# More gathered rows through ACT's DMA queue, in smaller blocks behind its long operations: a graph attention layer on Trainium2

## The chip, the cores and the metric

The kernel runs on one core of one Trainium2 chip. The metric is the device time of one execution in microseconds (us). PE is the matrix engine (PEld its weight loads), DVE the vector engine, ACT the scalar engine, POOL the general-purpose engine, SP the engine that issues most of the DMAs. ACT and POOL issue DMAs too, from their own instruction queues. A name with a q behind it (ACTq, SPq, POOLq) is the sequencer of that engine, which issues DMAs and loads registers.

## The reference

A graph has 12,500 nodes with 128 features and 200,000 edges, sorted by their destination. The layer normalizes the features and applies a relu (h), scores each edge, keeps at most the 16 best edges of each destination, and adds the messages of those with softmax weights:

```
h = relu(layernorm(x))
score = sum((h @ W_Q.T)[dst] * (h @ W_K.T)[src]) / sqrt(128) * exp(-edge_weight)
keep the 16 highest scores of each dst;  alpha = softmax of the kept ones by dst
agg[dst] += alpha * (h[src] @ W_msg.T)
out = x + relu(h @ W_self.T + agg)
```

All data are 32-bit floats or integers; the sources of the edges are random.

## The kernel before

**Tiles.** The edges stand in their order in chunks of 128, one edge to a partition. Fourteen chunks make a window (`GC = 14`), and there are 112 windows (`G`). A window's edges belong to a short run of nodes, so that the work between edges and nodes is done with one-hot matrices: `to_e` (nodes to edges), `opo` (places of an edge in its node's list of slots and in the window). A prologue normalizes x into the table `h_tab` in DRAM and prepares the indices.

**Rows of the sources.** Each edge needs the row of `h_tab` that belongs to its source, 512 bytes. They come by three ways:
- POOL gathers a whole chunk, 128 rows, with one indirect DMA (L183) into `hs`, a tile of a window with 8 buffers. `let_go` (L219) copies the chunk's indices on DVE and calls the gather; `more(k)` deals these calls out over a pass, two chunks each.
- SP takes chunk 13 of some windows, row by row, one DMA of 512 bytes each, 36 rows a pass (`SP_ROWS`), into `lateSP`.
- ACT takes chunk 12 of some windows in the same way, `ACT_ROWS` rows a pass, into `lateACT`. The chunks that these two streams take are fixed at build time: a stream with a rate of r rows a pass takes as many whole chunks as it can have ready in time. They are taken from POOL's work.

The row streams have two steps. `rows_named` loads up to 16 row numbers at a time into registers (L791). It is a generator: its body runs only as the loop over it asks for the next value. `rows_asked(name, n)` issues the next n DMAs (L803) from the numbers named so far. `all_landed` lets DVE wait for a chunk.

**The loop.** Pass i works on several windows at once, each in another stage, in an order written out by hand; the instructions of each engine run in that order. What this document speaks of:
- `far_of` (PE L602, ACT L604), four blocks, for window i+1. Its products lie in the one buffer "a" of PSUM, so each block's matmul waits for ACT to have read the block before. `to_edges` (ACT L609) makes `to_e` of it.
- `edges_turned` and `away` (PE L615 and L625, ACT L618 and L627), three blocks of `aw` in the same buffer, and `places` (ACT L631), which makes `opo`.
- `q_to_edges` (PE L642) and `scores` (DVE L653), four blocks of a window, window i.
- `slots_by_node` (PE L667 and L669) of window i-1, `best` (DVE from L683 on, the 16 best), `sum_of_exps` (ACT L700) and `kept_to_edges` (PE L712) of window i-2.
- `on_edges` (DVE L718 to L725), `exps` (ACT L729), `weights` (DVE L733, L734), then `sums` (PE L744, two halves) of window i-3, `sums_out` (ACT L749, tile `agn`), and for i-4 and i-5 the products, the output (DVE L764) and the store (SP L770).

A buffer of `hs` is free for a later window when the sums of its window are done.

Of the kernel before, what the change touches and what calls it, by code (L numbers as in the profile page):

```python
# [19 lines left out]
ACT = mybir.EngineType.Activation  # L20

SP_ROWS = 36
ACT_ROWS = 24
PSUM = bass.MemoryType.PSUM

P = 128
# [55 lines left out]
def gnn_layer(  # L82
# [106 lines left out]
    AT_ONCE = 16  # L189
    STREAMS = {"SP": (nc.sync, SP, -1, SP_ROWS, GC - 1), "ACT": (nc.scalar, ACT, 3, ACT_ROWS, GC - 2)}  # L190
    NLATE = 4
# [19 lines left out]
    def let_go(g, k):  # L211

        js = [j for j in range(2 * k, min(2 * k + 2, own[g])) if (g, j) not in slow]
        if k == 0:
            T[g]["ix"] = rows_pool.tile([P, GC], I32, name="ix", bufs=7)
        if not js:
            return
        ix, j0, j1 = T[g]["ix"], js[0], js[-1] + 1
        nc.vector.tensor_copy(ix[:, j0:j1], idx_all[:, GC * g + j0:GC * g + j1])  # L219
        gather(g, j0, j1, lambda j: ix[:, j:j + 1])  # L220
# [32 lines left out]
    def raw_stats(g):  # L253
        T[g]["raw"] = row_stats(rows_pool, T[g]["hs"], own[g], f"r{g % 2}")
# [5 lines left out]
    def raw_begun(g):  # L260
        normed(T[g]["hs"], 0, 1, *T[g]["raw"])

    def raw_finished(g, part):
        rows, (rs, sm) = T[g]["hs"], T[g]["raw"]
        if part < 3:
            normed(rows, 1 + 3 * part, 4 + 3 * part, rs, sm)
            return
        for t in range(10, own[g]):
            nc.vector.tensor_scalar(rows[:, t, :], rows[:, t, :], rs[:, t:t + 1], sm[:, t:t + 1],
                                    op0=OP.mult, op1=OP.add)  # L270
            nc.vector.tensor_scalar(rows[:, t, :], rows[:, t, :], 0.0, None, op0=OP.max)
# [256 lines left out]
    def softmax_rest(pool, v16):  # L528

        top = pool.tile([P, 1], F32, name="top")  # L530
        nc.vector.tensor_scalar(top, v16[:, 0:1], FLOOR, None, op0=OP.max)
        nm = pool.tile([P, 1], F32, name="nm")
        nc.vector.tensor_scalar(nm, top, -1.0, None, op0=OP.mult)
        e16 = pool.tile([P, TOPK], F32, name="e16")
        den = pool.tile([P, 1], F32, name="den")
        nc.scalar.activation(e16, v16, AF.Exp, bias=nm, accum_out=den)
        rden = pool.tile([P, 1], F32, name="rden")
        nc.vector.tensor_scalar(rden, den, 0.25, None, op0=OP.max)
        nc.vector.reciprocal(rden, rden)
        return top, e16, rden  # L540


    with tc.tile_pool(name="win", bufs=2) as win:
# [25 lines left out]
        def load_x(g):  # L569
            k = G - TAIL  # L570
            if g == k:
                starts(g, 1, TAIL, XT)
            T[g]["x_t"] = rows_pool.tile([P, D], F32, name="x_t", bufs=8)
            if g < k:
                nc.sync.dma_start(T[g]["x_t"], x[ds(T[g]["start", 0], P), :])
            else:
                nc.sync.dma_start(T[g]["x_t"], x_end[ds(T[g]["start", 1], P), :])
# [204 lines left out]
        def rows_named(name, i):  # L782

            _, engine, _, _, _ = STREAMS[name]
            todo = rows_at.get((name, i), [])
            while todo:
                g, j, e = todo[0]
                n = 1
                while n < min(AT_ONCE, len(todo)) and todo[n][:2] == (g, j):
                    n += 1  # L790
                _, numbers = nc.values_load_multi_w_load_instructions(  # L791
                    late_b[g:g + 1, j - GC + 2, e:e + n], engines=[engine], min_val=0, max_val=ROW * (N - 1),
                    skip_runtime_bounds_check_because="nodes' numbers times a row's bytes")
                ready[name] += [(g, j, e + k, st) for k, st in enumerate(numbers)]
                yield
                todo = todo[n:]

        def rows_asked(name, most=1000):
            for g, j, e, st in ready[name][:most]:
                m = slow[g, j][1]  # L800
                if e == 0:
                    T[g]["late", j] = win.tile([P, D], F32, name=f"late{name}", bufs=NLATE)
                d = STREAMS[name][0].dma_start(T[g]["late", j][e:e + 1, :].bitcast(U8), h_bytes[ds(st, ROW)])  # L803
                d.then_inc(landed[name][m % NLATE], 16)
                tc.no_tile_sem_insts.add(d.ins.name)
                tc.add_to_no_dep_group(f"rows{g}_{j}", d.ins)
            del ready[name][:most]
# [6 lines left out]
        def at(g, stage, *args):  # L814
            if 0 <= g < G:
                stage(g, *args)


        for i in range(-3, G - 1):
            at(i + 3, load_nodes)  # L820
            for k, _ in enumerate(rows_named("SP", i)):
                rows_asked("SP")
                if k == 0:
                    at(i - 1, load_x)
            if not rows_at.get(("SP", i)):
                at(i - 1, load_x)
            if i == G - 2:
                load_x(G - 2)
                load_x(G - 1)
            if i == 8:  # L830
                nc.sync.dma_start(h_tab[N:N + P, :], zpad)
                nc.sync.dma_start(x_end[XT:XT + P, :], zpad)
                nc.sync.dma_start(x_end[0:XT, :], x[N - XT:N, :])
            def raw(part):
                if i in (1, 2):
                    raw_finished(i + 1, part)

            def more(k):

                if i in (-1, 0, 1):  # L840
                    g = i + 6
                else:
                    g, k = (i + 4, k + 2) if k < 5 else (i + 5, k - 5)
                    if g < 8:
                        return
                if i >= -1 and g < G:
                    let_go(g, k)

            at(i, q_to_edges, 0)
            at(i - 5, output)  # L850
            at(i - 5, store)
            at(i - 3, weights)
            more(0)
            at(i - 4, sums_turned)
            at(i + 1, far_of, 0)
            at(i - 4, sums_turned_out)
            at(i + 1, q_out)
            at(i, q_to_edges, 1)
            at(i + 1, far_of, 1)
            rows_asked("ACT", ACT_ROWS // 8)  # L860
            raw(0)
            for b in range(3):
                at(i - 1, slots_by_node, b)
            at(i + 1, far_of, 2)
            more(1)
            at(i - 2, best)
            more(2)
            at(i - 2, sum_of_exps)
            at(i - 1, slots_out)
            raw(1)  # L870
            at(i, q_to_edges, 2)
            at(i + 1, far_of, 3)
            raw(2)
            at(i + 2, h_turned)
            at(i, scores, 0)
            more(3)
            at(i + 1, to_edges)
            rows_asked("ACT", ACT_ROWS * 5 // 16)
            at(i + 2, h_turned_out)
            at(i - 2, kept_to_edges)  # L880
            at(i - 1, node_by_slots)
            at(i + 1, edges_turned)
            at(i - 3, sums, 0)
            at(i, scores, 1)
            more(4)
            at(i + 1, away, 0)
            at(i, q_to_edges, 3)
            at(i - 2, one_over_sum)
            at(i + 1, away, 1)
            rows_asked("ACT")  # L890
            at(i - 3, sums, 1)
            at(i, scores, 2)
            at(i - 2, on_edges)
            more(5)
            at(i + 1, away, 2)
            at(i - 3, sums_out)
            at(i - 4, products)
            at(i - 2, exps)
            at(i + 1, places)
            for _ in rows_named("ACT", i + 1):  # L900
                pass
            rows_asked("ACT", ACT_ROWS * 3 // 8)
            at(i, scores, 3)
            at(i, scores_in_slots)
            if i == 0:
                raw_stats(2)
                raw_stats(3)
                raw_begun(2)
                raw_begun(3)
            if i in (1, 2):  # L910
                raw_finished(i + 1, 3)
            more(6)
            at(i + 2, q_made)
            if i > 0 and later:
                later.pop(0)()
# [92 lines left out]
    with tc.tile_pool(name="gen", bufs=1) as gen, tc.If(nc.values_load(  # L1008
# [116 lines left out]
        with tc.For_i(0, NT, 1) as T:  # L1125
# [16 lines left out]
            _, e16, rden = softmax_rest(gen, cand[:, 0:TOPK])  # L1142
# [40 lines left out]
```

## Time and profile before

| | us |
|---|---|
| median of 3 runs | 3100.45 |
| lowest and highest run | 3090.87, 3109.37 |
| profiled execution, its own time | 3112.28 |
| its span from the first to the last instruction | 3110.5 |

| in the profiled execution | count |
|---|---|
| gathers of POOL from `h_tab` | 1456 |
| row DMAs of SP, of ACT | 3968, 2560 |

The mean granted clock of PE is 0.741. Rows of a timeline give the start in us, the duration in us, engine, line, operation, tiles, shapes and count, and in brackets the idle time before it with what ended it. "issue" there is time in which the engine waited for nothing that the profile shows, "remote" an event that the profile can't put down to an instruction. Instructions of a sequencer aren't counted as busy time of its engine.

### The profile page before, as it was taken

How to read it: one execution, taken by the hardware profiler on the slowest of the kernel's cores; microseconds unless marked ns; L12 is line 12 of the kernel's file. 1: busy time of each engine (PE TensorE's matmuls, PEld its weight loads, DVE VectorE, ACT ScalarE, POOL GpSimd, SP SyncE). 2: the span in 40 equal slices, each digit the busy share in tenths (PEclk: the TensorE clock that was granted, in tenths of full speed). 3: DMA queues.
4: the chain of work that ended last, by engine and by line, in shares of the span. 5: the costliest groups of instructions: out<-in, count | busy, mean ns of one | idle time of the engine just before them, and what ended most of it. 6: DMA issues, size and time to landing. Idle time of an engine off the chain costs nothing. (4 is left out here: it accounts for less than half of the span.)

```text
span 3110.5 us, 55712 instructions
## 1 busy us (share of the span) xinstructions
PE 2052.1 (66%) x13800; PEld 1692.2 (54%) x13801; DVE 1264.1 (41%) x7016; ACT 1041.8 (33%) x2190; POOL 1457.7 (47%) x1529
## 2 busy tenths in 40 slices
PE   0256666666677667676676666776676666667667
PEld 0145555555555555555565555555565555555556
DVE  4453334433344334443433333434434433344346
ACT  4443323333333233333333333333333332333333
POOL 6524444444444444444444445444445444444440
PEclk9867777767777776777777777767767777777779
DMA  8201111111111111111111111111111111111110
GB/s 218 62 24 43 50 43 42 43 39 44 43 42 44 42 44 42 43 42 42 44 44 42 42 43 44 42 40 43 44 44 44 43 42 42 44 43 41 42 40 12
DMA packets 113004, 144.38 MB, mean 46 GB/s; under 512 B 36775, under 2 KB 86567, under 8 KB 111904
## 3 DMA queue, kind: packets, MB, share of 16 engines
q0 software_dynamic: 48512, 99.39, 12.6%
q1 hardware_dynamic: 59038, 40.04, 4.7%
q8 instruction: 109, 1.79, 0.2%
q14 instruction: 225, 1.84, 0.2%
q10 hardware_dynamic: 5120, 1.32, 0.2%
HBM read 126.79 MB, written 14.40 MB: 45 GB/s over the span
## 5 line engine op out<-in xcount | busy, mean ns | idle before, releaser
L183 POOL DMA_INDIRECT hs<-h_tab,ix x1456 | 1394.9, 958 | 1540.6 <-PE e L744 605.4
L744 PEld LDWEIGHTS e<-hs,alz 128*128 128x128 f32 x3142 | 612.1, 296 | 291.9 <-issue 280.5
L744 PE MATMUL e<-hs,alz 128*128 128x128 f32 x3142 | 668.9, 393 | 0.0
L642 PE MATMUL q<-q,to_e 128*128 128x128 f32 x3348 | 589.9, 324 | 44.9 <-issue 42.9
L642 PEld LDWEIGHTS q<-q,to_e 128*128 128x128 f32 x3348 | 545.9, 234 | 121.5 <-issue 87.5
L604 ACT ACTIVATE far<-a,minus 128x512 bf16<-128x512 f32 (+1 forms) x447 | 294.6, 659 | 891.9 <-issue 344.2
L653 DVE SCALAR_TENSOR_TENSOR prod<-hs,dec_all,q 128x128 f32<-128x128 f32 x1623 | 470.2, 342 | 133.6 <-remote 60.1
L602 PE MATMUL a<-rel,ident 112*128 112x512 bf16 (+1 forms) x447 | 211.0, 472 | 426.0 <-issue 264.4
L627 ACT ACTIVATE aw<-a 128x400 bf16<-128x400 f32 x336 | 169.4, 504 | 836.7 <-PE a L625 450.4
L683 DVE TENSOR_SCALAR ell<-slots,e 128x40 f32<-128x40 f32 x112 | 27.9, 249 | 933.6 <-remote 390.2
L625 PE MATMUL a<-minus_at,pdT 32*128 32x400 bf16 x336 | 146.6, 436 | 376.1 <-ACT aw L627 245.4
L669 PE MATMUL e<-opo,sl 128*41 128x40 f32 x3348 | 236.9, 252 | 34.0 <-issue 33.9
L669 PEld LDWEIGHTS e<-opo,sl 128*41 128x41 f32 x3348 | 215.7, 168 | 43.5 <-issue 31.3
L667 PEld LDWEIGHTS <-zrow 1*41 1x41 bf16 x112 | 11.3, 101 | 412.3 <-issue 412.2
L609 ACT ACTIVATE to_e<-far 128x1920 f32<-128x1920 bf16 x112 | 201.3, 1797 | 3.4
L764 DVE SCALAR_TENSOR_TENSOR o<-s,x_t 128x128 f32<-128x128 f32 x112 | 32.6, 291 | 403.2 <-ACT up L729 350.1
L625 PEld LDWEIGHTS <-pdT 32*128 32x128 bf16 x336 | 31.4, 94 | 190.5 <-ACT pdT L618 122.9
L631 ACT ACTIVATE opo<-aw 128x1200 f32<-128x1200 bf16 x112 | 134.7, 1202 | 0.1
L653 DVE DVE_READ_ACCUMULATOR prod<-hs,dec_all,q 128x1 f32 x1623 | 132.0, 81 | 0.0
L219 DVE COPY ix<-idx_all 128x2 int32<-128x2 int32 (+1 forms) x747 | 126.1, 183 | 0.0
L712 PEld LDWEIGHTS <-to_e 128*128 128x128 bf16 x1674 | 68.0, 111 | 94.4 <-DVE km L695 88.0
L712 PE MATMUL x<-km,to_e 128*128 128x43 bf16 x1674 | 76.7, 202 | 58.4 <-DVE km L695 58.3
(197 smaller groups left out, 1868.0 us busy)
## 6 DMA issues: line engine op xcount, KB each, us to landing
lateSP<-h_tab SPq DMA_DIRECT2D x3968, 0.5 KB
lateACT<-h_tab ACTq DMA_DIRECT2D x2560, 0.5 KB
hs<-h_tab,ix POOLq DMA_INDIRECT x1456
h_r<-h_tab SPq DMA_DIRECT2D x112, 64.0 KB
x_t<-in_x_dram SPq DMA_DIRECT2D x108, 64.0 KB
out_dram<-o SPq DMA_DIRECT2D x108, 64.0 KB
xg<-in_x_dram SPq DMA_DIRECT2D x2, 1400.0 KB
h_tab<-xg SPq DMA_DIRECT2D x2, 1400.0 KB
```

What stands on the lines that cost most here:

```text
L183: nc.gpsimd.indirect_dma_start(out=T[g]["hs"][:, j, :], out_offset=None, in_=table[0:N, :], in_offset=bass.IndirectOffsetOnAxis(ap=index(j ...
L602: nc.tensor.matmul(pr[:, 0:n1 - n0], lhsT=upper(ident[0:RR, g:g + 1]).to_broadcast([RR, P]), rhs=rel[:, n0:n1], start=True, stop=True)
L604: nc.scalar.activation(T[g]["far"][:, n0:n1], pr[:, 0:n1 - n0], AF.Square, bias=minus)
L609: nc.scalar.activation(T[g]["to_e"][:, 0:n], T[g]["far"][:, 0:n], AF.Relu, bias=1.0, scale=-1.0)
L625: nc.tensor.matmul(pr[:, 0:400], lhsT=T[g]["pdT"], rhs=minus_at.rearrange("k w j s -> k (w j s)")[:, n0:n1], start=True, stop=True)
L627: nc.scalar.activation(T[g]["aw"][:, n0:n1], pr[:, 0:400], AF.Square)
L631: nc.scalar.activation(T[g]["opo"].rearrange("e w j s -> e (w j s)"), T[g]["aw"], AF.Relu, bias=1.0, scale=-1.0)
L642: nc.tensor.matmul(pq[:, (j - j0) * P:(j - j0 + 1) * P], lhsT=T[g]["to_e"][:, j * P:(j + 1) * P], rhs=T[g]["q"], start=True, stop=True)
L653: nc.vector.scalar_tensor_tensor(prod, rows_of(g, j), dec_all[:, c:c + 1], T[g]["pq", b][:, (j % 4) * P:(j % 4 + 1) * P], op0=OP.mult, op1 ...
L669: nc.tensor.matmul(et[0:KM + 1, STEP * j:STEP * j + WN], lhsT=sl1[g % 2][:, j, :], rhs=T[g]["ow"][:, j, :], start=False, stop=(j == n - 1))
L712: nc.tensor.matmul(px[:, j, 0:KM + 3], lhsT=upper(T[g]["to_e"][:, j * P:(j + 1) * P]), rhs=upper(T[g]["km"]), start=True, stop=True)
L744: nc.tensor.matmul(T[g]["pa"], lhsT=alz[g % 2][:, WW * j + PRE:WW * j + PRE + P], rhs=rows_of(g, j), start=(j == 0), stop=(j == n - 1))
```

## The change

`ACT_ROWS` goes from 24 to 40. In the loop, the calls of `rows_asked("ACT", ...)` are dealt out anew; the numbers are ACT's row DMAs at each place of a pass:

| place in ACT's order | before | after |
|---|---|---|
| behind `far`, block 0 | 0 | 3 |
| behind `far`, block 1 | 3 | 3 |
| behind `far`, block 2 | 0 | 3 |
| behind `to_e` | 7 | 7 |
| behind `aw`, block 0 | 0 | 3 |
| behind `aw`, block 1 | 5 (all that are left) | 3 |
| behind `aw`, block 2 | 0 | 3 |
| behind `opo` and the loads of the next numbers | 9 | 15 |

```diff
-ACT_ROWS = 24
+ACT_ROWS = 40
...
             at(i + 1, far_of, 0)
+            rows_asked("ACT", 3)
             at(i - 4, sums_turned_out)
             at(i + 1, q_out)
             at(i, q_to_edges, 1)
             at(i + 1, far_of, 1)
-            rows_asked("ACT", ACT_ROWS // 8)
+            rows_asked("ACT", 3)
...
             at(i + 1, far_of, 2)
+            rows_asked("ACT", 3)
             more(1)
...
             at(i + 1, to_edges)
-            rows_asked("ACT", ACT_ROWS * 5 // 16)
+            act_names = rows_named("ACT", i + 1)
+            rows_asked("ACT", 7)
...
             at(i + 1, away, 0)
+            rows_asked("ACT", 3)
...
             at(i + 1, away, 1)
-            rows_asked("ACT")
+            rows_asked("ACT", 3)
...
             at(i + 1, away, 2)
+            rows_asked("ACT", 3)
             at(i - 3, sums_out)
             at(i - 4, products)
             at(i - 2, exps)
             at(i + 1, places)
-            for _ in rows_named("ACT", i + 1):
+            for _ in act_names:
                 pass
-            rows_asked("ACT", ACT_ROWS * 3 // 8)
+            rows_asked("ACT", ACT_ROWS - 25)
```

## The prediction

> **What bounds the kernel now.** I read the page first, then the busy time of two stretches, then the waits by engine, and last the timeline of single passes, because the page's averages name no bound: no engine is busy for more than two thirds.
>
> ```profile
> span 3110.5 us, 55712 instructions
> PE 2052.1 (66%) x13800; PEld 1692.2 (54%) x13801; DVE 1264.1 (41%) x7016; ACT 1041.8 (33%) x2190; POOL 1457.7 (47%) x1529
> 1519.00:1546.50 27.50, 18.37 (x124) 15.29 (x123) 10.65 (x61) 8.68 (x19) 13.43 (x15) 0.75 0.16 40
> 3020.20:3038.20 18.00, 14.34 (x127) 12.12 (x124) 9.57 (x52) 8.70 (x18) 0.00 (x0) 0.88 0.07 17
> ```
>
> The last two rows are two stretches, each one pass of the main loop (us, then busy time and count of PE, weight loads, DVE, ACT and POOL, then granted clock, DMA share and GB/s). Both hold the same matrix, vector and scalar work and both issue 24 rows on ACT. The first also has POOL's gathers and lasts 27.5 us, the second comes after the last gather and lasts 18.0. So a pass is longer than its work by what goes on around the gathers. The waits (engine, line, what it waited for, us in total, times, longest) say where:
>
> ```profile
> POOL hs L183 <- PE e L744: 605.4, 99, 7.9
> POOL hs L183 <- issue: 370.0, 1210, 0.6
> DVE ell L683 <- remote: 390.2, 44, 9.9
> ACT far L604 <- issue: 344.2, 126, 4.3
> DVE ell L683 <- PE a L602: 267.9, 30, 9.2
> DVE ell L683 <- PE e L669: 225.9, 29, 9.4
> PEld L667 <- issue: 412.2, 111, 5.7
> PE a L602 <- ACT far L604: 161.2, 106, 17.2
> ```
>
> POOL itself waits, for a buffer that the sums (L744) free, so it isn't the bound by its own rate. But `best` (L683), with which the second half of a pass begins on DVE, is often released by something other than the matmuls it needs (L669): 74 of 103 times in these three rows. And PE waits some 3.7 us in each pass ahead of L667 (412.2 over 111), after its L602 has waited for ACT's `far`. One pass shows both:
>
> ```profile
> 1504.56 0.95 POOL L183 DMA_INDIRECT hs<-h_tab,ix  x1 [7.72 <-PE e L744]
> 1505.19 0.51 ACT L627 ACTIVATE aw<-a 128x400 bf16<-128x400 f32 x1 [3.65 <-PE a L625]
> 1505.59 0.36 ACT L749 ACTIVATE agn<-e,rden 128x128 f32<-128x128 f32 x1
> 1505.94 1.20 ACT L631 ACTIVATE opo<-aw 128x1200 f32<-128x1200 bf16 x1
> 1507.77 3.27 ACTq L803 DMA_DIRECT2D lateACT<-h_tab  x9
> 1508.70 7.56 SPq L803 DMA_DIRECT2D lateSP<-h_tab  x12
> 1511.09 0.69 ACT L604 ACTIVATE far<-a,minus 128x512 bf16<-128x512 f32 x1 [3.94 <-issue]
> 1511.83 0.38 PE L602 MATMUL a<-rel,ident 112*128 112x512 bf16 x1 [3.53 <-ACT far L604]
> 1512.30 2.32 PE L669 MATMUL e<-opo,sl 128*41 128x40 f32 x30
> 1513.60 0.94 POOL L183 DMA_INDIRECT hs<-h_tab,ix  x1 [0.30 <-issue]
> 1516.26 0.25 DVE L683 TENSOR_SCALAR ell<-slots,e 128x40 f32<-128x40 f32 x1 [8.64 <-PE a L602]
> 1518.66 0.94 POOL L183 DMA_INDIRECT hs<-h_tab,ix  x1 [4.11 <-DVE prod L653]
> ```
>
> Two chains leave from about 1504.5, where the sums end. On POOL, eight gathers start at 1504.56, 1.25 us apart, the eighth ending at 1514.54; `best` starts 1.72 us after that. On ACT, `aw`, `agn`, `up`, `opo`, then two loads of row numbers and nine row DMAs, and only then `far` at 1511.09; PE's L602 waits for that `far`, and L669 follows and ends at 1514.62. The gathers' chain ends last, by 1.64 us. From `best` on, a second burst of up to six gathers starts (1518.66), and the next sums stand behind it. Where there are no gathers, ACT's chain ends last:
>
> ```profile
> 3026.88 0.50 ACT L627 ACTIVATE aw<-a 128x400 bf16<-128x400 f32 x1 [1.75 <-PE a L625]
> 3027.28 0.36 ACT L749 ACTIVATE agn<-e,rden 128x128 f32<-128x128 f32 x1
> 3027.63 1.20 ACT L631 ACTIVATE opo<-aw 128x1200 f32<-128x1200 bf16 x1
> 3029.37 2.90 ACTq L803 DMA_DIRECT2D lateACT<-h_tab  x9
> 3032.32 0.69 ACT L604 ACTIVATE far<-a,minus 128x512 bf16<-128x512 f32 x1 [3.48 <-issue]
> 3033.53 1.48 PE L669 MATMUL e<-opo,sl 128*41 128x40 f32 x30
> 3035.05 0.25 DVE L683 TENSOR_SCALAR ell<-slots,e 128x40 f32<-128x40 f32 x1 [6.05 <-PE e L669]
> ```
>
> Here `best` starts 0.04 us after L669, and `far` 0.05 us after the ninth DMA (3029.37 + 2.90 = 3032.27). So ACT's compute instruction stands behind the whole block of issues in its queue.
>
> **The change part by part.** Rows on ACT go from 24 to 40 a pass. ACT's stream takes one whole chunk (128 rows) at a time: 20 chunks now (2560 rows), 33 after (4224).
>
> *What POOL loses.* Thirteen gathers of 1456. One costs 0.96 us busy and 0.31 us of issue (370.0 over 1210), and they fall in the second burst, which is on the path: 13 x 1.26 = 16 us less in all. DVE loses a copy or a part of one with each; it idles there.
>
> *Rows placed under long operations.* Three behind the first `far`, three (as now) behind the second, three behind the third, seven (as now) behind `to_e`, three behind the first `aw`, three instead of five behind the second. A row costs 2.90/9 = 0.32 us of ACT's queue. Behind the first `far`, `aggT`, `q` and the second `far` start up to 0.3 us later; PE has L669 to do meanwhile, so nothing. Behind the third, the next on ACT is the exponential that needs `best`'s result, later than three rows take. Behind the first two `aw`, PE has q's block and the second half of the sums. All these I cost at nothing; should the cover go, three rows are 0.96 us a pass.
>
> *Three rows behind the last `aw`.* Ahead of `agn`, `up` and `opo`, with no matmul that hides it: `agn` now starts 0.40 us after `aw` (3026.88 to 3027.28), then not before three rows are issued, 0.95 us. Term A: +0.5 us on ACT's chain. DVE's `kept` and `o` wait for `up` and move with it, well ahead of their use on PE (the next sums).
>
> *The block behind `opo`.* The numbers are still loaded there, since the generator that holds the loads runs only when the loop over it does. Forty numbers in loads of at most 16 are three loads, not two, and then 15 DMAs, not nine.
>
> ```profile
> L791 ACTq TENSOR_LOAD <-late_b x213: 551/1041/1241, 215.0 to 3045.1; - x107
> ```
>
> The row is one line's durations in ns (min/median/max). The longer ones overlap `opo`, so the third load costs near the minimum. Term B: +0.6. Six more DMAs at 0.32: term C, +1.9.
>
> *Rows that fall into the gathers' flight.* With A to C the block ends some 9.5 us after the burst's start instead of 6.5. In that stretch, issues can be slow:
>
> ```profile
> 2131.85 3.46 ACTq L803 DMA_DIRECT2D lateACT<-h_tab  x3
> 3033.53 0.83 ACTq L803 DMA_DIRECT2D lateACT<-h_tab  x3
> 2129.47 9.36 SPq L803 DMA_DIRECT2D lateSP<-h_tab  x16
> 2131.84 1.37 PE L669 MATMUL e<-opo,sl 128*41 128x40 f32 x30
> 2136.37 0.25 DVE L683 TENSOR_SCALAR ell<-slots,e 128x40 f32<-128x40 f32 x1 [8.14 <-remote]
> ```
>
> Three rows behind the second `far`, issued while a burst was in flight, took 3.46 us; with no burst 0.83. SP pays 0.58 to 0.63 a row there (9.36/16, 7.56/12), against 0.32. So the block's last rows, four or five of them, cost more. Bounds for term D: 0 and 2.6 us (3.46 - 0.83). I take 1.4, five rows at SP's surplus of 0.28, which is about the middle, as the fast and the slow case both occur.
>
> *The sum.* A + B + C + D = 0.5 + 0.6 + 1.9 + 1.4 = 4.4 us later `far`, and so L669. Of that the gathers' chain already covers what L669 now waits for in vain: 1.64 us in the pass of 1504, 3.16 in that of 2131 (2136.37 - 2133.21), none in the 29 waits that end with L669. Three quarters at 2.4 make 1.8; I take 1.7. Net 2.7 us a pass. POOL's first burst doesn't move against the sums, and its second follows `best`, so the whole of it goes into the period. Forty rows a pass run in 105 passes. The last gather starts at 3018.9, so three of them have no burst: there A + B + C = 3.0 counts whole. 102 x 2.7 + 3 x 3.0 - 16 = 275 + 9 - 16 = +268 us. The profiled execution took 3112.3 us for its span of 3110.5, 0.4% over the median of 3100.45, inside the runs' spread; 3100 + 268 gives **3370 us** as forecast (3112 + 268 = 3380 against the profile).
>
> [...] The trace agrees that L669 comes at two prices, 2.32 us (1512.30) and 1.48 (3033.53). [...]
>
> **The rivals.** *The block is not slowed* (D = 0). For it: ACT's nine rows of 1507.77 were issued at 0.36 while SP paid 0.63. Against: the 3.46. Then 1.3 net: 102 x 1.3 + 9 - 16 = +126, 3225 us.
>
> *The burst holds all late rows* (D = 2.6). For it: SP is slow in every burst shown. Against: the same block of three cost 0.83 without one. Net 3.9: 102 x 3.9 - 7 = +391, 3490 us; L669 at 2.32 instead of 1.48 where it is fast now could add a few tens of us.
>
> *Issues cost ACT nothing, and the gathers decide* (faster). If ACT's compute instructions could be taken up while its queue issues DMAs, neither the third load nor the six rows would hold `far`; the gathers' chain would keep ending last, and 13 gathers fewer would be the whole effect: 3100 - 16 = 3084 us. It decides as soon as `far` comes no later than the 1.6 us of slack. Against it: `far` at 3032.32 right behind the ninth issue, and 126 waits of `far` put down to issue. [...]
>
> *It doesn't move the path* (no change): the rows' cost just fills the slack, 1.7 us, and the gathers' saving stays small. A + B + C alone are 3.0, so this needs half of them hidden.
>
> **How the numbers follow.** Forecast 0.70, rows not slowed 0.11, rows held 0.12, gathers decide 0.04, no change 0.03. The range runs from the first rival's price, 3225, to 3520, 30 us beyond the second's for L669's slower price; it leaves out the cases at and below no change (0.07) and the far ends. A difference of 0.5% (16 us) is about what a measurement of this kernel can tell from none. Slower by more than that: 0.93; within: 0.03; faster: 0.04.
>
> **What would show it.** In the changed profile: ACT's block behind `opo` has 15 issues and takes 5 to 8 us (now 3); `far` starts some 4 us later after the first gather of its burst, near 11 us instead of 6.5; PE's wait ahead of L667 roughly doubles from 3.7 us a pass; `best` is released by L669, not later than it; the first burst's eight gathers stay 1.25 us apart; a pass lasts about 30 us. Wrong would be: `far` starting before the block has been issued, `best` still 1.7 to 2 us behind the eighth gather with L669 long done, or a period that grew while that block didn't.

## The result: slower, 3543 us for 3099

| | before | after |
|---|---|---|
| median, us | 3098.74 | 3543.01 |
| lowest and highest run, us | 3090.87, 3109.37 | 3533.71, 3566.31 |
| profiled execution: its time, its span, us | 3112.28, 3110.5 | 3566.31, 3564.6 |
| gathers from `h_tab` | 1456 | 1443 |

The ratio is 1.1442, 95% interval 1.1373 to 1.1512. The change makes the kernel slower, as forecast, but by 444 us where 268 were forecast; 3543 lies 23 us above the range.

The changed kernel's page, two lines of it:

```profile
span 3564.6 us, 59136 instructions
PE 1911.8 (54%) x13800; PEld 1593.3 (45%) x13801; DVE 1273.6 (36%) x7012; ACT 1069.6 (30%) x2190; POOL 1447.9 (41%) x1516
```

No engine works much longer than before: ACT 28 us more, DVE 10, PE 140 less. The time has gone into waits. The waits of the changed kernel (engine, line, what it waited for, us in total, times, longest):

```profile
DVE ell L683 <- PE e L669: 1345.0, 108, 13.7
PEld L667 <- issue: 1041.6, 111, 11.1
...
PE a L602 <- ACT far L604: 950.4, 107, 14.6
ACT far L604 <- issue: 942.4, 110, 10.0
```

`best` (L683) is now released by L669 108 times; before it was 29. PE's wait ahead of L667 has gone from 3.7 to 9.4 us a pass (1041.6 over 111), and `far` waits 942 us for ACT's own issues, before 344. One pass of the changed kernel's timeline:

```profile
1712.55 0.95 POOL L183 DMA_INDIRECT hs<-h_tab,ix  x1 [6.09 <-PE e L744]
1712.81 0.50 ACT L627 ACTIVATE aw<-a 128x400 bf16<-128x400 f32 x1 [3.16 <-PE a L625]
1712.88 0.83 ACTq L803 DMA_DIRECT2D lateACT<-h_tab  x3
1713.75 0.37 ACT L749 ACTIVATE agn<-e,rden 128x128 f32<-128x128 f32 x1 [0.44 <-issue]
...
1714.12 1.19 ACT L631 ACTIVATE opo<-aw 128x1200 f32<-128x1200 bf16 x1
...
1716.15 8.44 SPq L803 DMA_DIRECT2D lateSP<-h_tab  x12
...
1716.92 8.06 ACTq L803 DMA_DIRECT2D lateACT<-h_tab  x15
...
1721.39 0.95 POOL L183 DMA_INDIRECT hs<-h_tab,ix  x1 [0.30 <-issue]
...
1725.03 0.69 ACT L604 ACTIVATE far<-a,minus 128x512 bf16<-128x512 f32 x1 [9.72 <-issue]
...
1726.53 2.32 PE L669 MATMUL e<-opo,sl 128*41 128x40 f32 x30
...
1728.89 0.25 DVE L683 TENSOR_SCALAR ell<-slots,e 128x40 f32<-128x40 f32 x1 [13.49 <-PE e L669]
```

The eighth gather ends at 1722.34, as early after the first as before. The block of 15 is issued until 1724.98, `far` follows 0.05 us later, and `best` comes 0.04 us behind L669 (1726.53 + 2.32 = 1728.85). ACT's chain ends last now.

Means over the passes that have a burst of eight gathers (96 before, 97 after; all 104 of each give the same within 0.03), worked out from the rows of the timelines, in us:

| | before | after |
|---|---|---|
| last `aw` to `agn` | 0.40 | 0.95 |
| end of `opo` to ACT's first row | 0.60 | 1.60 |
| the block behind `opo` | 3.02 | 7.32 |
| first gather to `far` | 6.21 | 12.09 |
| end of L669 to `best` (what L669 waits for in vain) | 1.78 | 0.04 |
| first gather to `best` | 11.78 | 15.94 |
| period | 26.87 | 31.24 |

### The profile page after: what moved, and what is told of

Read it like the earlier page. It is cut to its first block, busy times and chain, and to the rows that moved or that the text cites. A ratio compares the mean times of both kernels' runs of the same rounds, so it can differ in the third digit from the quotient of the medians.

```text
span 3564.6 us, 59136 instructions
## 1 busy us (share of the span) xinstructions
PE 1911.8 (54%) x13800; PEld 1593.3 (45%) x13801; DVE 1273.6 (36%) x7012; ACT 1069.6 (30%) x2190; POOL 1447.9 (41%) x1516
## 5 line engine op out<-in xcount | busy, mean ns | idle before, releaser
L602 PE MATMUL a<-rel,ident 112*128 112x512 bf16 (+1 forms) x447 | 221.5, 496 | 996.3 <-ACT far L604 950.4
L744 PEld LDWEIGHTS e<-hs,alz 128*128 128x128 f32 x3116 | 509.6, 253 | 253.7 <-issue 245.9
L642 PE MATMUL q<-q,to_e 128*128 128x128 f32 x3348 | 565.9, 322 | 0.0
L744 PE MATMUL e<-hs,alz 128*128 128x128 f32 x3116 | 561.7, 347 | 0.0
L642 PEld LDWEIGHTS q<-q,to_e 128*128 128x128 f32 x3348 | 537.9, 234 | 43.0 <-issue 22.3
L683 DVE TENSOR_SCALAR ell<-slots,e 128x40 f32<-128x40 f32 x112 | 27.9, 249 | 1348.9 <-PE e L669 1345.0
L667 PEld LDWEIGHTS <-zrow 1*41 1x41 bf16 x112 | 12.1, 108 | 1041.7 <-issue 1041.6
L669 PE MATMUL e<-opo,sl 128*41 128x40 f32 x3348 | 254.7, 267 | 0.0
L669 PEld LDWEIGHTS e<-opo,sl 128*41 128x41 f32 x3348 | 238.3, 185 | 14.7
L618 ACT CAST pdT<-a 32x128 bf16<-32x128 f32 x112 | 28.5, 254 | 226.8 <-remote 225.0
L725 DVE TENSOR_REDUCE kept<-mine 128x15 f32<-128x600 f32 x112 | 86.9, 776 | 14.6 <-DVE mine L723 10.6
```

Of the source, the lines that this page charges most:

```text
L602: nc.tensor.matmul(pr[:, 0:n1 - n0], lhsT=upper(ident[0:RR, g:g + 1]).to_broadcast([RR, P]), rhs=rel[:, n0:n1], start=True, stop=True)
L642: nc.tensor.matmul(pq[:, (j - j0) * P:(j - j0 + 1) * P], lhsT=T[g]["to_e"][:, j * P:(j + 1) * P], rhs=T[g]["q"], start=True, stop=True)
L669: nc.tensor.matmul(et[0:KM + 1, STEP * j:STEP * j + WN], lhsT=sl1[g % 2][:, j, :], rhs=T[g]["ow"][:, j, :], start=False, stop=(j == n - 1))
L744: nc.tensor.matmul(T[g]["pa"], lhsT=alz[g % 2][:, WW * j + PRE:WW * j + PRE + P], rhs=rows_of(g, j), start=(j == 0), stop=(j == n - 1))
```

## The experiments

The theories: BLOCK (what ACT issues between the last `aw` and the first `far` sets the end as soon as it is longer than the gathers' chain) against COUNT (the number of rows a pass matters), SMALL BLOCKS (the thin dealing itself matters) and ACT BOUND (ACT's chain set the end before, too). For the price of a row in the block there are SLOWED BY GATHERS and SLOWED BY SP (SP's rows do it), and for what makes rows slow while gathers run, later, RUN (a long run of rows), IN FLIGHT (rows still under way) and OFFSET (the time since the first gather). Ratios are to the kernel before on the same chip, with 95% intervals. That kernel took 3106 to 3146 us on the chips of the first eight and the last three runs, and 2186 and 2188 us on those of the seven between, which turned out to matter. Ratios of runs on different chips differ by the chip, too (1.1442 and 1.1794 for the change).

**The three rows behind the last `aw`** are moved behind the second.

```diff
             at(i + 1, away, 1)
-            rows_asked("ACT", 3)
+            rows_asked("ACT", 6)
...
             at(i + 1, away, 2)
-            rows_asked("ACT", 3)
+            rows_asked("ACT", 0)
```

> The changed kernel, with the three rows that stand behind the last aw, ahead of agn, moved behind the second aw (six there, none behind the third). Theory BLOCK (what ACT must issue between the last aw and far decides): far comes 0.55 us earlier (agn starts 0.40 us after aw instead of 0.95), and a little more as one or two rows less fall into the gathers' flight: 0.55 to 1.1 us in 102 passes, so 3430 to 3490 us. Rival COUNT (each of the 16 further rows a pass costs the same wherever it stands on ACT's queue): nothing changes, 3543 us.

3540.66 us, ratio 1.1275 [1.1241, 1.1309], against 1.1442 for the change. `agn` is back at 0.40 us behind `aw`, but `far` comes only 0.09 us earlier (12.00), since the block takes 7.68 us instead of 7.32. What the rows gave back at one place, the block behind them took most of. BLOCK's gain of 0.55 us or more was missed. The time is the one that COUNT expected, but the kernel before is 47 us slower on this chip, and so the run doesn't decide between the two.

**Forty rows, the block nine again**, six more behind the second `aw`.

```diff
             at(i + 1, away, 1)
-            rows_asked("ACT", 3)
+            rows_asked("ACT", 9)
...
-            rows_asked("ACT", ACT_ROWS - 25)
+            rows_asked("ACT", 9)
```

> The changed kernel, still 40 rows a pass, with the block behind opo cut from 15 to 9 rows and the six put behind the second aw (nine there, where ACT then waits over 3 us for the sums). BLOCK: the block takes 3.0 us again instead of 7.3, far comes about 8 us after the burst's first gather (12.1 in the changed kernel, 6.2 before), L669 ends about when the gathers let best go (11.8), so a pass is again bound by the gathers: 3095 to 3160 us. COUNT: still 3543 us. Rival SMALL BLOCKS (the three rows each behind far 0, far 2 and the first aw cost it): at least 3400 us, since those stay.

3186.59 us, ratio 1.0137 [1.0116, 1.0158]. Its timeline (the ninth row goes out behind the start of `far`):

```profile
1705.22 3.14 ACTq L803 DMA_DIRECT2D lateACT<-h_tab  x8
...
1708.64 0.69 ACT L604 ACTIVATE far<-a,minus 128x512 bf16<-128x512 f32 x1 [5.08 <-issue]
...
1710.13 2.32 PE L669 MATMUL e<-opo,sl 128*41 128x40 f32 x30
...
1712.49 0.25 DVE L683 TENSOR_SCALAR ell<-slots,e 128x40 f32<-128x40 f32 x1 [8.83 <-PE e L669]
```

BLOCK's 3095 to 3160 us were for a kernel before of 3099 us; 1.0137 of that are 3141. The same forty rows and three loads cost a tenth of what the change costs. So it isn't the count, and the small blocks, all still there, aren't it either: six rows at one place are.

**Twenty-four rows dealt out thinly**, with two behind `opo`.

```diff
-ACT_ROWS = 40
+ACT_ROWS = 24
...
             at(i + 1, away, 2)
-            rows_asked("ACT", 3)
+            rows_asked("ACT", 0)
...
-            rows_asked("ACT", ACT_ROWS - 25)
+            rows_asked("ACT", 2)
```

> 24 rows a pass as before, dealt out in small blocks: three behind each of far 0, 1 and 2, seven behind to_e, three behind the first and second aw, none behind the third, and two (before: nine) behind opo. BLOCK with the gathers' chain ending last before the change: far comes some 2.2 us earlier than before, but best still starts 11.8 us after the burst's first gather, so the time stays within 1% of before: 3080 to 3130 us; L669 ends 3 to 4 us ahead of best instead of 1.8. Rival ACT BOUND (ACT's block was the bound before too): 2.2 us less in 102 passes, about 2870 us. SMALL BLOCKS: slower than before by over 2%.

3125.58 us, ratio 0.9928 [0.9905, 0.9951]. `far` comes 3.97 us after the first gather, 2.2 us earlier than before, and `best` at 11.82 as before: the other chain ends last, although ACT's is shorter by 2.2 us, and ACT BOUND is out on this chip.

**The changed kernel, and the kernel before, without gathers** and index copies from window 16 on. Line numbers in these two are three higher.

```diff
-        js = [j for j in range(2 * k, min(2 * k + 2, own[g])) if (g, j) not in slow]
+        js = [j for j in range(2 * k, min(2 * k + 2, own[g])) if (g, j) not in slow or 8 <= g < 16]
+        if g >= 16:
+            T[g]["hs"] = T[g - 8]["hs"]
+            return
```

From window 16 on a window uses the rows of the window eight before, so the output is another; windows 8 to 15 gather all their chunks for that.

> The changed kernel without POOL's gathers, and without the copies of their indices, from window 16 on: these windows use the rows of the window eight before (so the output is another). Theory SLOWED BY GATHERS: the block of 15 takes 15 x 0.32 = 4.8 us instead of 7.3, far follows at once, and a pass takes about 20.5 to 21.5 us (17.5 to 18 for a pass without gathers before, plus 3.0 to 3.5 of the rows and the third load): about 2450 to 2550 us. Rival SLOWED BY SP (SP's row DMAs, not the gathers, slow ACT's issues): the block still takes over 6.5 us, a pass 22.5 us or more, over 2600 us.

> The kernel before without gathers and their index copies from window 16 on (its output is therefore another); to be set against the changed kernel without gathers, whose pass took 22.8 us and whose time was 0.867 of the kernel before. ROWS (the sixteen further rows and the third load cost ACT's path the same whether gathers run or not, only less each): without gathers the two kernels differ by A + B + C, 0.55 + 1.0 + 1.9 = 3.5 to 4.5 us a pass; this kernel's pass is 18 to 19.5 us, the block of nine takes 2.9 to 3.1 us, the time is 2250 to 2370 us. GATHERS ONLY (the rows cost something only when gathers are in flight): the difference is under 1.5 us, the pass 21.5 to 23, the time 2600 to 2730. LATE RELEASES (what PE has done is passed on late while gathers are in flight): the waits for PE that the trace cannot put down to an instruction disappear here, and best starts right behind L669 (0.05 us).

2727.91 us, ratio 0.8674 [0.8654, 0.8694], and 2325.57 us, 0.7392 [0.7368, 0.7416]. First the changed kernel's rows, then the other's:

```profile
1507.22 5.16 SPq L806 DMA_DIRECT2D lateSP<-h_tab  x16
1508.15 4.92 ACTq L806 DMA_DIRECT2D lateACT<-h_tab  x15
...
1513.12 0.69 ACT L607 ACTIVATE far<-a,minus 128x512 bf16<-128x512 f32 x1 [6.72 <-issue]
```

```profile
1503.92 3.19 ACTq L806 DMA_DIRECT2D lateACT<-h_tab  x9
1505.41 5.58 SPq L806 DMA_DIRECT2D lateSP<-h_tab  x16
1507.15 0.69 ACT L607 ACTIVATE far<-a,minus 128x512 bf16<-128x512 f32 x1 [3.88 <-issue]
```

With SP issuing beside it the block of 15 takes 4.92 us, 4.89 in the mean of the passes: without gathers no row is slowed (0.33 us a row). That is the block of SLOWED BY GATHERS, but not its time (2450 to 2550 us); the time is in the range of SLOWED BY SP (over 2600), whose block of over 6.5 us didn't come. The block decides, since the time was worked out from too short a pass: it is 22.3 us, because `far` still stands behind `opo`, three loads and 15 rows. The second gives ROWS: from the last `aw` to `far` it is 5.60 us there and 9.05 here, 3.45 more, and the pass 3.8 more (18.5 and 22.3). What LATE RELEASES expected of the waits came, too: `best` waits for "remote" once there (10.0 us), 44 times in the kernel before (390.2 us).

**The loads of the numbers**, with the three rows of the first experiment, behind the second `aw`.

```diff
...
             at(i + 1, away, 1)
-            rows_asked("ACT", 3)
+            rows_asked("ACT", 6)
+            for _ in rows_named("ACT", i + 1):
+                pass
...
             at(i + 1, places)
-            for _ in act_names:
-                pass
-            rows_asked("ACT", ACT_ROWS - 25)
+            rows_asked("ACT", 15)
...
```

> The changed kernel with the three rows behind the last aw and the three loads of row numbers both moved behind the second aw (the first of these two moves alone gave 3540.7 us, ratio 1.1275 on this chip). TERM B (the three loads stand on the path, 1.6 to 1.7 us between the end of opo and the first row): the first row comes 0.1 to 0.3 us behind opo, far some 1.5 us earlier after the first gather (12.0 to 10.5), the ratio is 1.07 to 1.09. TERM D (rows cost more the later they stand in the gathers' flight): as above, and the block of fifteen falls from 7.7 to some 6.5 us because it starts 1.5 us earlier, far at 9 to 9.7, ratio 1.03 to 1.06. COVER (the idle time ahead of the last aw, 3.65 us, does not hold six rows and three loads, 1.9 + 2 to 3.1 us): the last aw, and with it agn and opo, come later by what is over, and the ratio is 1.09 to 1.13.

3452.58 us, ratio 1.0990 [1.0957, 1.1023].

```profile
1711.61 0.50 ACT L627 ACTIVATE aw<-a 128x400 bf16<-128x400 f32 x1 [4.46 <-PE s L588]
...
1712.22 0.45 ACTq L803 DMA_DIRECT2D lateACT<-h_tab  x1
...
1712.37 1.20 ACT L631 ACTIVATE opo<-aw 128x1200 f32<-128x1200 bf16 x1
1712.77 8.72 ACTq L803 DMA_DIRECT2D lateACT<-h_tab  x14
1721.54 0.69 ACT L604 ACTIVATE far<-a,minus 128x512 bf16<-128x512 f32 x1 [7.97 <-issue]
```

COVER held: six rows and three loads don't fit, and the last `aw` starts 1.7 us after the first gather instead of 0.6. The rest wasn't expected. The rows go out from 1.35 us before the end of `opo` (the first one, at 1712.22, even ahead of its start), so the issues begin some 3 us earlier against `opo` than in the first experiment; yet the block gets longer, 8.58 us from its first row on. In the change rows were slow from about 7 us after the first gather. Here they are slow from 5. What agrees instead is the mean time from one row of the block to the next by its number: 0.55 us for the first step in every kernel, then 0.31 to 0.43 up to the seventh, and from the eighth on mostly 0.65 to 1.2 in both, until about 11 us after the first gather.

**No rows through SP.**

```diff
-SP_ROWS = 36
+SP_ROWS = 0
```

> The changed kernel with no rows through SP's queue: POOL gathers SP's 31 chunks as well. GATHERS (the rows of ACT's block are slowed by the gathers in flight alone): the block of fifteen still takes 7 to 7.7 us, far 11.8 to 12.3 us after the first gather; 31 gathers more in the second burst at 1.3 to 2.1 us add 40 to 65 us to the changed kernel's time, ratio 1.155 to 1.17. SP (ACT's and SP's issues slow each other while gathers run): the block takes 4.8 to 5.5 us, far comes some 2 us earlier, and the ratio is 1.08 to 1.11.

3459.76 us, ratio 1.1001 [1.0969, 1.1033], with 31 gathers more. The block takes 6.45 us, between the two expectations, though the ratio is in SP's range; its eighth to eleventh steps take 0.64 to 0.76 us, in the change 0.74 to 0.97. So gathers slow ACT's rows without any row of SP, and SP's rows add about a third of the whole (6.45 less 4.89 is 1.56 us, 7.32 less 4.89 is 2.43). Which of the two queues holds the other is seen in no run here.

**Nine rows ahead of `agn` and nine behind `opo`**, run three times.

```diff
             at(i + 1, away, 2)
-            rows_asked("ACT", 3)
+            rows_asked("ACT", 9)
...
-            rows_asked("ACT", ACT_ROWS - 25)
+            rows_asked("ACT", 9)
```

> The changed kernel with its eighteen rows between the last aw and far dealt out as nine behind the last aw, ahead of agn, and nine behind opo (three and fifteen before). In the changed kernel the first seven rows of the block cost 0.31 us each and the rest 0.7 to 1.0, in the kernel whose block starts 2.3 us earlier after the first gather too (there the eighth row falls at 5.5 us, in the changed kernel at 8.0). RUN (only a run of more than some eight rows is slowed; two runs of nine with opo and three loads between them are not): no row over 0.4 us on the mean, agn 2.8 us behind aw, far 9.6 to 10.2 us after the first gather, ratio 1.06 to 1.09. IN FLIGHT (about eight rows can be under way while the gathers are; those of the first run still count): the second run is slow from its first rows on, far 11.3 to 12.3, ratio 1.12 to 1.145. OFFSET (rows are slow from 7 to 11 us after the first gather, whatever went before): the second run, from 7 us on, is slow, far 11.3 to 12.3, the first run fast.

> The kernel with nine rows behind the last aw and nine behind opo once more; on the chip where the kernel before took 2186 us it had no row over 0.33 us and could not tell its theories apart. On a chip where the kernel before takes some 3100 us: RUN: no row over 0.4 us on the mean, far 9.3 to 10.2 us after the first gather, ratio 1.06 to 1.09. IN FLIGHT: the second run slow from its first rows on, far 11.3 to 12.3, ratio 1.12 to 1.145. OFFSET: first run fast, rows of the second slow from 7 us on, far 11.3 to 12.3, the same ratio. Where the kernel before takes some 2190 us: 1.17 again.

> Nine rows behind the last aw and nine behind opo a third time, in the hope of a chip on which the kernel before takes some 3100 us. There: RUN: no row over 0.4 us on the mean, far 9.3 to 10.2 us after the first gather, ratio 1.06 to 1.09. IN FLIGHT: the second run slow from its first rows on, far 11.3 to 12.3, ratio 1.12 to 1.145. OFFSET: first run fast, rows of the second slow from 7 us on, far 11.3 to 12.3. Where the kernel before takes some 2190 us: 1.175 again.

The first two, 2568.68 us (1.1746 [1.1715, 1.1777]) and 2572.18 us (1.1753 [1.1732, 1.1774]), fell on chips on which no row is slowed (none over 0.33 us in the first; on the chip of the second the change's block of fifteen takes 4.90 us, as without gathers). The third, of two timings, was 3363.39 us, ratio 1.0833 [1.0794, 1.0872]. Its timeline:

```profile
1704.78 0.94 POOL L183 DMA_INDIRECT hs<-h_tab,ix  x1 [7.44 <-PE e L744]
...
1705.10 2.66 ACTq L803 DMA_DIRECT2D lateACT<-h_tab  x9
...
1710.96 3.77 ACTq L803 DMA_DIRECT2D lateACT<-h_tab  x8
1715.00 0.69 ACT L604 ACTIVATE far<-a,minus 128x512 bf16<-128x512 f32 x1 [5.63 <-remote]
```

This is nearest to RUN: behind their first step the second nine go at 0.31 to 0.42 us a row up to 8.4 us after the first gather, by when the change's rows were slow, so IN FLIGHT and OFFSET are out as they were put. But the steps that end at 8.9 and 9.9 us take 0.51 and 0.97, so "no row over 0.4" was missed by these two, the sixth and seventh of the run, and `far` comes at 10.3 us, just past RUN's range. A fixed count of eight it is not. The ninth row goes out behind the start of `far` here. In 67 of 90 passes of this run `far` starts before the end of the block's last row, by up to 2.0 us, in the change in 10 of 99, by up to 1.1; on the other kind of chip, where no row is slowed, it stands 0.05 us behind it in all 99. So one held row was overtaken in some of these passes, two in none. The same 18 rows and three loads are on ACT's path in both kernels, and cutting the run in two takes the ratio from 1.1442 to 1.0833, though the first nine now hold `agn` by 2.4 us. The pause between the two runs is 3.2 us in the mean. What a shorter one does, the kernel before shows, where three rows follow the block of nine: in its 104 passes with a burst they took 2.6 to 3.5 us in all four with a pause of at most 1 us, and 0.8 to 3.5 us where it was 1 to 2 us (under 1 us in 31 of 66).

**The changed kernel on the other kind of chip.**

> The changed kernel once more, beside the next ones. The kernel before took 3099 to 3146 us on the chips of the earlier runs and 2186 us on the chip of the last three. If the kernel before takes some 3100 here: 1.12 to 1.15 as before. If it takes some 2190: ROWS ALONE (no row is slowed there, A + B + C = 0.55 + 1.0 + 1.9 = 3.45 us in each of 105 passes, no slack, 13 gathers at 1.26 us less): 340 to 360 us more, 2530 to 2550 us, ratio 1.155 to 1.165; SAME LOSS (rows are slowed there as well): 440 us more, ratio 1.20.

2580.95 us, where the kernel before took 2188.31: ratio 1.1794 [1.1774, 1.1814], 393 us, between ROWS ALONE (340 to 360) and SAME LOSS (440). Its timeline, and the line of the waits that `best` has left:

```profile
1720.49 0.94 POOL L183 DMA_INDIRECT hs<-h_tab,ix  x1 [0.30 <-issue]
1720.51 5.20 SPq L803 DMA_DIRECT2D lateSP<-h_tab  x16
1720.99 4.79 ACTq L803 DMA_DIRECT2D lateACT<-h_tab  x15
...
1725.49 0.94 POOL L183 DMA_INDIRECT hs<-h_tab,ix  x1 [0.30 <-issue]
1725.83 0.69 ACT L604 ACTIVATE far<-a,minus 128x512 bf16<-128x512 f32 x1 [6.39 <-issue]
```

```profile
DVE ell L683 <- PE e L669: 1095.8, 108, 10.8
```

The block is issued amid gathers, which start every 1.25 us, and no row is slowed: it takes 4.90 us in the mean, the price without gathers. The pass is 22.35 us, also that of the changed kernel without gathers.

**Versions that might beat both.** Forty rows with the loads behind the second `far`; thirty-two rows in three dealings; twenty-four once more. Rows behind the three `far`, `to_e`, the three `aw` and `opo`:

```
the change, 40 rows: 3 3 3, 7, 3 3 3, 15
40 rows: 3 3 3, 9, 3 10 0, 9, loads behind the second far
32 rows: 0 3 3, 7, 3 9 0, 7
32 rows: 0 6 6, 7, 0 11 0, 2
32 rows: 3 6 5, 7, 3 6 0, 2
24 rows: 3 3 3, 7, 3 3 0, 2
```

> Forty rows with nothing behind the last aw, the loads of the numbers behind the second far, nine rows behind to_e, ten behind the second aw, nine behind opo. PATH (only what ACT issues between the last aw and the first far counts, and there it is less than in the kernel before by the two loads): far comes 5 to 6 us after the first gather, best is set by the gathers again (11.8 us after the first), and what remains of the change is thirteen gathers fewer in the second burst, where one is worth 1.3 to 2.1 us by the passes with five and with six of them: 17 to 27 us less than the kernel before, ratio 0.985 to 0.995. MOVED ELSEWHERE (the loads behind the second far hold the exponential of best's result, or the ten rows the last aw): the second half of a pass grows by 1 to 2 us, ratio 1.02 to 1.06.

> Thirty-two rows (26 chunks, six gathers fewer than in the kernel before): none behind the first far, three behind the second and the third, seven behind to_e, three behind the first aw, nine behind the second, none behind the last, seven behind opo; two loads of numbers behind opo as in the kernel before. PATH (what ACT issues between the last aw and the first far counts, here two rows less than in the kernel before): far some 5.6 us after the first gather, the gathers set best (11.8 us), six gathers fewer at about 2 us each: 12 us less than the kernel before, with what the 24 rows dealt out thinly gained (ratio 0.9928) 0.985 to 0.997. SECOND HALF (rows behind to_e, the first and the second aw hold the sums, as with the forty rows at 1.016): ratio 1.00 to 1.015.

> Thirty-two rows with two behind opo (and two loads), none behind the first far and the first aw, six behind the second and the third far, seven behind to_e, eleven behind the second aw. PATH: far some 4 us after the first gather, the gathers set best, and six gathers fewer: ratio 0.983 to 0.993, better than the 24 rows dealt out thinly (0.9928). SECOND HALF (eleven rows behind the second aw take 3.5 us, as long as the idle time there, and rows behind the third far hold the exponential): ratio 1.00 to 1.02.

> Thirty-two rows with two behind opo and eleven behind the second aw once more (0.981 on the chip where the kernel before took 2186 us). On a chip where it takes some 3100: PATH: far 4 to 5.5 us after the first gather, best set by the gathers (11.8 us), ratio 0.98 to 0.993. SECOND HALF: ratio 1.00 to 1.02.

> Twenty-four rows dealt out thinly, two behind opo, once more (0.9928 on a chip where the kernel before took 3146 us). There again 0.99 to 0.995. On a chip where the kernel before takes some 2190 us ACT's chain has no slack, and seven rows fewer in front of far are worth 7 x 0.32 = 2.2 us in each of 105 passes: 200 to 235 us less, ratio 0.89 to 0.91, if nothing else becomes the bound; if the gathers or the second half take over, 0.92 to 0.97.

> Thirty-two rows, two behind opo, eleven behind the second aw. Where the kernel before takes some 3100 us: PATH 0.98 to 0.993, SECOND HALF 1.00 to 1.02. Where it takes some 2190: 0.98 again.

> Thirty-two rows as 3, 6, 5 behind the first three far, 7 behind to_e, 3 and 6 behind the first two aw, none behind the last, 2 behind opo. Where the kernel before takes some 2190 us: with the 24 rows dealt out thinly (0.9245) POOL issues gathers almost without a pause, with 11 rows behind the second aw (0.979) the last aw comes late; here neither six rows (1.9 us) nor three hold an aw, and six gathers fewer at 1.25 us each take 8 us off: ratio 0.915 to 0.925; if the added rows hold the second half, 0.93 to 0.97. Where it takes some 3100: 0.98 to 0.993 if the gathers' chain sets the end, 1.00 to 1.01 if the second half grows.

| | before at 3106 to 3146 us | before at 2186 to 2188 us |
|---|---|---|
| 40 rows, loads behind `far` | 1.0160 [1.0137, 1.0183] | |
| 32 rows, 7 behind `opo` | | 1.0253 [1.0229, 1.0277] |
| 32 rows, 11 behind the second `aw` | 0.9941 [0.9919, 0.9963] | 0.9808 [0.9785, 0.9831], 0.9789 [0.9765, 0.9814] |
| 32 rows, 3 6 5, 7, 3 6 0, 2 | 0.9925 [0.9897, 0.9953] | |
| 24 rows, 2 behind `opo` | 0.9928 [0.9905, 0.9951] | 0.9245 [0.9229, 0.9261] |

The forty rows lost in the way of MOVED ELSEWHERE, with a ratio just under its 1.02 to 1.06. `far` came at 4.42 us, but nine rows behind `to_e` fell into the second burst's flight, took 3.54 us in the mean where seven took 2.08, and held the copies that the next matmuls need:

```profile
1726.20 3.96 ACTq L803 DMA_DIRECT2D lateACT<-h_tab  x9
...
1730.20 0.27 ACT L585 COPY hT<-s 128x128 f32<-128x128 f32 x1 [2.26 <-remote]
```

The first dealing of 32 rows missed both of its expectations, which were worked out from the passes of a chip with some 3100 us. On its own chip the last `aw` has less cover: ACT's idle time ahead of it is 1.74 us in the changed kernel and with the 24 rows, where on the other kind of chip it is 3.3. The nine rows take 2.65; 32 numbers cost 1.07 us behind `opo` where 24 cost 0.60. The same holds for the eleven rows (3.25 us). Where the kernel before takes over 3100 us, the best versions take 0.7% off it, and the further eight rows bring nothing that can be told (0.9925 is within PATH's 0.98 to 0.993, 0.9941 just past it). Where it takes 2190, twenty-four rows take 7.6% off: there ACT's chain sets the end of a pass (`best` stands 0.04 us behind L669 in every trace from such a chip; the kernel before has none), and the thin dealing shortens it. It is faster than both kernels on both kinds, by 0.7% on the one.

## Why the prediction was right in its sign and too low

*What bounds the kernel, and the slack.* Right as to which chain ends last and by how much: the slack was taken as 1.7 us and is 1.74 (1.78 less 0.04). ACT's chain ends last at fifteen rows behind `opo`, the other at two or nine. That the gathers themselves hold `best` isn't shown: on the other kind of chip it follows L669 by 0.04 us, with gathers 1.25 us apart there, too (last section).

*Term A*, +0.5: measured +0.55.

*Term B*, +0.6, the third load: mis-sized, measured +1.0 (1.60 less 0.60). I took the least duration of a load, arguing that only `opo` stretches the longer ones. But the second load grew, too, from eight numbers to sixteen, and the third is the one of eight. The price goes by the numbers loaded: 0.60 us behind `opo` for 24, 1.07 to 1.09 for 32 (two loads as well), 1.60 for 40. The changed kernel's loads show the two prices, a load of eight near the least and one of sixteen at the median:

```profile
L791 ACTq TENSOR_LOAD <-late_b x317: 534/1043/1333, 213.9 to 3483.2; - x159
```

*Term C*, +1.9: measured 1.92 without gathers (4.89 less 2.97 us of block, means).

*Term D*, +1.4, bounds 0 and 2.6: the step that failed. The block grew by 4.3 us, so D is 4.3 - 1.9 = 2.4, near its upper bound. I took five late rows at SP's mean surplus of 0.28. But that mean holds quick steps and slow ones: in the kernel before, the third to seventh steps of SP's runs take 0.73 to 1.09 us in the mean, those from the ninth on 0.33 to 0.36. So it is with ACT's block: behind the first, its steps up to the seventh take 0.31 to 0.43 us, the next four 0.74 to 0.97, a surplus of 0.4 to 0.65 each, and the later ones little. The 3.46 us of three rows was rightly taken as rare (in the 104 passes these three rows take 0.88 us in the median, 1.36 in the mean, 3.49 at most), but it is no bound for a block of fifteen; that D came out below it is luck. The rival that holds all late rows, 3490 us, had D nearly right and was still 53 us too low, since it has B as small.

*The sum.* A + B + C + D are 0.55 + 1.0 + 1.9 + 2.4 = 5.9; less 1.74 that is 4.1, and `best` is measured 4.16 us later, the period 4.37. 102 times 4.37 are 446 us, with the 13 gathers' saving in it; measured 444. Of the 176 us by which the forecast fell short, D has 102 and B 41 (102 times 1.0 and 0.4). The rest is mostly the second half of a pass, 0.2 us longer (21 us), which I had taken 16 us shorter in all for the gathers. The range's upper end took D at 2.6 and added 30 us for L669, but nothing for B.

*The order of ACT's queue, and L669.* The compute instruction behind the row issues waited again: `far` at 1725.03 stands 0.05 us behind the fifteenth row, as in 89 of 99 passes. In the other ten it starts ahead of the end of that row, but behind the fourteenth, so it gained one row at most. The other way round ACT's sequencer did run ahead, since rows went out while `opo` ran (1712.77 in the run with the loads moved). No run shows the 30 us that the range had for a slower L669: it takes 2.32 us after, in every pass with a burst, where PE has been idle for 7.3 to 10.4 us ahead of L602, and 2.43 in the mean before, where only seven of 104 passes have it at 1.37 (PE idle for 2.3 to 2.5 us); so its slower price added next to nothing here.

*The gathers' saving.* 16 us for 13 gathers rested on 1.26 us each. Passes of the kernel before with five gathers in the second burst have a second half of 13.99 us, those with six 16.10 (means of 33 and 57 passes, from `best` to the next burst): one is worth 2.1, which changes the sum by 11 us.

## What to carry to other kernels

In this kernel a block of DMA issues on ACT was priced by its place and its length (forty rows with fifteen behind `opo`: 1.1442 and 1.1275; with nine there: 1.0137): find the chain on which such a block lies, and what slack that chain has, before adding to it. Take the slowed price of an issue from rows that are slow (0.74 to 0.97 us here), not from the mean of a run that is part fast (0.58 to 0.63), and count the numbers to be loaded, not the loads (0.60 us behind `opo` for 24, 1.07 for 32 in two loads as well). Measure on more than one chip (2186 and 3146 us here) when waits appear that the profile can't put down to an instruction.

## What the runs showed of the hardware that I had not expected

**Where the kernel before takes some 3100 us, row DMAs were slowed while gathers were in flight, the late ones of a long run most.** In the runs of fifteen that begin 2.3 and 4.7 us after the first gather, some seven or eight issues go at 0.31 us and the rest at 0.65 to 1.2, until about 11 us after the first gather. It is no fixed count: nine rows behind nine others slow down from their sixth step on (0.51 us, then 0.97), and SP's runs in the kernel before from their third (0.73 to 1.09). What holds the rows (how many may be under way) was not seen in the trace and stays open.

**The same kernel takes 2186 us on some chips and 3099 to 3146 on others.** Two chips were of the first kind, and one of the others was met twice, an hour apart, both times at over 3100 us. On the first kind no row is slowed, and the waits that the profile puts down to "remote" are gone: none is left in any of the seven runs there, while the kernel before has, among others:

```profile
DVE ell L683 <- remote: 390.2, 44, 9.9
...
ACT aw L627 <- remote: 326.3, 64, 6.0
ACT far L604 <- remote: 316.9, 80, 17.3
```

On the other kind `best` stands 1.78 us behind L669's end in the mean of the passes with gathers in flight, and of these waits, 44, 64 and 80, the kernel before without gathers has 1, 4 and 7 left. So whether what I called the gathers' chain is a chain of gathers at all was not shown. PE's granted clock differs as well, 0.88 for the kernel before on the first kind and 0.74 on the other; but it is 0.86 on the other, too, without gathers, and so isn't set by the chip alone. Why `best` comes so late behind L669 on some chips wasn't settled. The change loses on both kinds, 444 and 393 us: 1.1442 and 1.1794.
